# Gram stages of a two-layer bottleneck kernel: a quarter of each copy step by ScalarE, twelve transfers a step for sixteen, norms a step further ahead

## The chip, the cores and the metric

The kernel runs on one core of one Trainium2 chip. The metric is device time in microseconds (us) of one execution; the median of three runs stands for a kernel. All numbers here are from runs of this kernel on the chip and from one execution that the hardware profiler recorded.

## What is computed

Two ResNet bottleneck layers, one after the other, on x of 64 images x 1024 channels x 14 x 14 pixels (float32, 12544 pixels in all), with batch statistics taken over all images and pixels:

```python
out = relu(bn(conv(x, w1, 1x1), g1, be1))        # 1024 -> 256 channels
out = relu(bn(conv(out, w2, 3x3), g2, be2))      # 256 -> 256
out = bn(conv(out, w3, 1x1), g3, be3)            # 256 -> 1024
x = relu(x + softplus(residual_scale)[0] * out)  # then the same again with layer 1's weights
```

`bn` subtracts the mean of a channel over images and pixels, divides by sqrt(variance + 1e-5), and applies g and be.

## The kernel before, in words

The 256 channels between the convolutions live on chip in one array, `y_all`: 128 partitions, `MS` = 2 channels a partition ("slots"), 12544 pixels along the partition. The program runs in stages: the first 1x1 convolution of layer 0; for each layer the 3x3 convolution (`conv2`), then a Gram stage (`gram`, L994), then `conv3_stats` (L1099), which makes from the Gram matrix the statistics that the third normalization needs, and then the last 1x1 convolution (with layer 1's first 1x1 convolution beside it in layer 0). There are two Gram stages, one a layer.

The statistics of conv3's output, a linear map of y, follow from y's mean and its 256 x 256 Gram matrix. `gram` therefore needs y with pixels on the partitions: TensorE contracts over partitions. A `zt` tile holds 2 x 128 pixels (`CH` = 2) by 256 channels and a column of ones; six of them (`NZT`) are used in turn. Two products per 128 pixels go into the PSUM banks `cp` and `ap` (L1092, L1093), for all 49 tiles, always one tile behind the making of the tiles. A tile is made in one of two ways:

- `by_tensor` (L1035): TensorE transposes four 128 x 128 blocks into PSUM, and VectorE copies them out (L1046). The first seven tiles (`FIRST`) are made so.
- `by_vector` (L1049): VectorE transposes 32 x 32 blocks inside each group of 32 partitions (L1052). That alone would leave the pixels in groups of 32 on the wrong partitions, so the data are moved beforehand: `spread(k)` (L1024) copies a step of 1536 pixels (`STEP` = 4 runs of `RUN` = 384) from `y_all` into a buffer `home` by sixteen transfers, one for each pair (i, j): run i of the channels in partition group j goes to partition group i, column block j. Each transfer moves 32 partitions x 2 slots x 384 pixels (96 KB). Nine of the sixteen are issued by SyncE (SP), seven by GpSimd (POOL). For i = j the data keep their partitions. There are seven steps (`STEPS`), and two buffers in turn (named `ws` and `home` in layer 0, `home` twice in layer 1), so `spread(k + 2)` waits until VectorE has transposed step k. A step feeds six tiles.

Before a pixel can be used, conv2's normalization must be applied to it: `norm_to(end)` (L1012) takes the next pieces of `y_all` (`bounds`, L1006: 256, 512, 1536, 832 and then 1568 pixels) up to `end`. For each piece and slot ScalarE applies scale, shift and ReLU (`norm`, L541, its instruction is L544) and VectorE then adds a per-channel constant (`less`, L1009, L1010). Slot 1 of the first piece is done by VectorE alone (L550, L552). This is 19 ScalarE instructions in a Gram stage.

What sets the order: `pairs` (L1059) is a generator that makes tiles and calls `norm_to` and `spread` in between, at places written out by hand (`then`, L1062, during the first seven tiles; after each step's six tiles from then on). VectorE's and TensorE's instructions here keep their program order; ScalarE's norms are placed by the scheduler, which left them in program order. Each engine then runs its own queue in order: a VectorE instruction that waits for a norm holds back all VectorE work behind it, and a transfer that waits holds back those behind it on its queue. In `spread`, `norm_to(first + STEP)` comes first, so that the step's own pixels are normalized before they are moved.

The last lines that the steps of the prediction touch: L168 is the helper through which all products go; L1107 is ScalarE's first work after a Gram stage (it takes the result out of PSUM), and L331 is the helper `act`, which issues a ScalarE instruction in program order.

Of the kernel before, what the change touches and what calls it, by code (L numbers as in the profile page):

```python
# [38 lines left out]
AF = mybir.ActivationFunctionType  # L39
# [7 lines left out]
MS = M // P  # L47
# [10 lines left out]
RUN = 3 * P  # L58
STEP = 4 * RUN
# [7 lines left out]
GPX = GI * HW  # L67
# [20 lines left out]
def bottlenecks(ctx: ExitStack, tc: tile.TileContext, x, w1s, w2s, w3s, pars, out):  # L88
    nc = tc.nc
# [5 lines left out]
    y_all = keep.tile([P, MS, NPX], FP, tag="y", name="y")  # L95
# [70 lines left out]
    def matmul(*args, **kw):  # L166

        tc.keep_in_program_order(nc.tensor.matmul(*args, **kw))  # L168

    def busy(psum, tag, n, with_=None):  # L170

        v = ident if with_ is None else with_
        for i in range(n):
            matmul(psum.tile(448, tag), v, v[:, :1].to_broadcast([P, 448]), start=True, stop=True)
# [154 lines left out]
    def act(*args, **kw):  # L329

        tc.keep_in_program_order(nc.scalar.activation(*args, **kw))  # L331
# [209 lines left out]
    def norm(s, y, aff, act=nc.scalar.activation):  # L541

        scale, shift = aff
        act(y, y, AF.Relu, bias=shift[:, s : s + 1], scale=scale[:, s : s + 1])  # L544

    def norm_vector(s, y, aff, less=0.0):

        scale, shift = aff
        tc.keep_in_program_order(
            nc.vector.tensor_scalar(y, y, scale[:, s : s + 1], shift[:, s : s + 1], ALU.mult, ALU.add)  # L550
        )
        tc.keep_in_program_order(nc.vector.tensor_scalar(y, y, 0.0, less, ALU.max, ALU.add))  # L552
# [441 lines left out]
    def gram(psum, pool, homes, aff, minus_c, beside):  # L994

        g0, g1 = psum.tile(M + 1, "cp"), psum.tile(P + 1, "ap")
        zts = [pool.tile([P, CH, M + 1], FP, tag=f"zt{i}", name=f"zt{i}") for i in range(NZT)]
        for zt in zts:  # L1000
            nc.gpsimd.memset(zt[:, :, M:], 1.0)
        zts = itertools.cycle(zts)

        head = 3 * CH * P
        start = FIRST * CH * P
        bounds = [0, CH * P, head, head + STEP, *range(2 * GPX, NPX + 1, GPX)]  # L1006
        pieces = list(zip(bounds, bounds[1:]))

        def less(s, y):  # L1009
            tc.keep_in_program_order(nc.vector.tensor_scalar(y, y, minus_c[:, s : s + 1], None, ALU.add))  # L1010

        def norm_to(end):  # L1012

            while pieces and pieces[0][0] < end:
                a, e = pieces.pop(0)
                for s in reversed(range(MS)):
                    y = y_all[:, s, a:e]
                    if a == 0 and s == 1:
                        norm_vector(s, y, aff, minus_c[:, s : s + 1])
                    else:  # L1020
                        norm(s, y, aff)
                        less(s, y)

        def spread(k):  # L1024

            first = start + k * STEP if k else head
            norm_to(first + STEP)
            x = homes[k % 2][:, : MS * STEP].rearrange("p (s j f) -> p s j f", s=MS, j=4)
            for i, j in itertools.product(range(4), range(4)):
                queue = nc.gpsimd if 4 * i + j in (1, 3, 6, 8, 10, 13, 15) else nc.sync  # L1030
                a = first + i * RUN
                queue.dma_start(out=x[32 * i : 32 * i + 32, :, j], in_=y_all[32 * j : 32 * j + 32, :, a : a + RUN])
            return x.rearrange("p s j f -> p (s j) f")

        def by_tensor(a):  # L1035
            tp = psum.tile(CH * M)
            for c in range(CH):
                for s in range(MS):
                    tc.keep_in_program_order(
                        nc.tensor.transpose(  # L1040
                            tp[:, (c * MS + s) * P : (c * MS + s + 1) * P],
                            y_all[:, s, a + c * P : a + (c + 1) * P], ident,
                        )
                    )
            zt = next(zts)
            tc.keep_in_program_order(nc.vector.tensor_copy(zt[:, :, :M], tp.rearrange("p (c m) -> p c m", c=CH)))  # L1046
            return zt

        def by_vector(x, i):  # L1049
            zt = next(zts)  # L1050
            tc.keep_in_program_order(
                nc.vector.transpose(  # L1052
                    zt[:, :, :M].rearrange("p b (n c) -> p b n c", c=32),
                    x[:, :, i * CH * 32 : (i + 1) * CH * 32].rearrange("p n (b r) -> p b n r", r=32),
                )
            )
            return zt

        def pairs():  # L1059

            norm_to(head)
            then = {  # L1062
                1: lambda: ready.append(spread(0)),
                2: partial(norm_to, 2 * GPX),
                4: partial(norm_to, 3 * GPX),
                5: lambda: ready.append(spread(1)),
            }
            for i in range(FIRST):
                a = i * CH * P
                yield by_tensor(a if a < head else a + STEP)  # L1070
                if i == 0:
                    busy(psum, "ax", 1)
                if i in then:
                    then[i]()
            for k in range(STEPS):
                x = ready.pop(0)
                for i in range(RUN // (CH * 32)):
                    yield by_vector(x, i)
                if k + 2 < STEPS:
                    ready.append(spread(k + 2))  # L1080
            norm_to(NPX)
            for i in range(LAST):
                yield by_tensor(NPX - (LAST - i) * CH * P)

        ready = []
        total = NPX // (CH * P)
        before = None
        for k, zt in enumerate(itertools.chain(pairs(), (None,))):
            if before is not None:
                for c in range(CH):  # L1090
                    first, last = k == 1 and c == 0, k == total and c == CH - 1
                    matmul(g0, before[:, c, 0:P], before[:, c, :], start=first, stop=last)  # L1092
                    matmul(g1, before[:, c, P:M], before[:, c, P:], start=first, stop=last)  # L1093
            before = zt
            if k in beside:
                beside[k]()
        return g0, g1
# [133 lines left out]
    def aggregate(stats, first):  # L1231
        n = stats.shape[1]
        mv = small.tile([P, n, nc.vector.BN_AGGR_DIM], FP, tag=f"mv{n}", name="mv")
        for o in range(n):
            tc.keep_in_program_order(
                nc.vector.bn_aggr(mv[:, o, :], stats[:, o, first:, :].rearrange("p t f -> p (t f)"))
            )
        return mv
# [93 lines left out]
    with tc.tile_pool(name="first", bufs=1) as one, tc.tile_pool(  # L1332
# [5 lines left out]
        for b in range(2):  # L1338
            p = keep.tile([P, NPAR], FP, tag=f"par{b}", name=f"par{b}")
# [31 lines left out]
    for b in range(2):  # L1371
# [7 lines left out]
        with tc.tile_pool(name=f"last_{b}", bufs=1) as one, tc.tile_pool(  # L1379
# [5 lines left out]
            aff = affine(aggregate(stats2, 0), pb, G2, BE2)  # L1385
            with ExitStack() as scope:
# [4 lines left out]
                with tc.tile_pool(name=f"gram_{b}", bufs=1) as pool:  # L1391
                    def x_tile(name):
                        return xpool.tile([P, CS * PX], FP, tag="x", name=name)


                    ws = sums_tile(one, 2 - b)
                    homes = [x_tile("home") if b else ws.rearrange("p i n -> p (i n)"), x_tile("home")]

                    weights = []

                    def combined():
                        if b == 0:
                            weights.append(combine_w1(w1, ws[:, 1]))
                        weights.append(combine_w3(w3, ws[:, 0]))

                    beside = {FIRST + STEPS * RUN // (CH * 32): combined}
                    grams = gram(psum, pool, homes, aff, minus_c, beside)

                    made = [conv3(psum, 0, 0, w3, "cx" if b else "ay")]
                    mv3 = small.tile([P, CS, nc.vector.BN_AGGR_DIM], FP, tag="mv3", name="mv3")  # L1410
                    conv3_stats(psum, pool, grams, w3, mv3, ("cy", "cp", "cy", "cp" if b else "cx"), homes[1])
# [3 lines left out]
                aff = affine(mv3, pb, G3, BE3, conv_bias=B3)  # L1415
# [51 lines left out]
```

## Time and profile before

| | us |
|---|---|
| median of 3 runs | 1944.43 (1944.18 to 1944.73) |
| the profiled execution | 1944.06 |
| its span on the core | 1942.3 |
| first Gram stage, first transpose to last product | 587.8 to 659.3 |
| second Gram stage, the same | 1553.3 to 1624.3 |
| ScalarE's 19 norms in the first stage | 586.5 to 612.6 |

| 586 to 604 us | busy us of 18 | | 604 to 660 us | busy us of 56 |
|---|---|---|---|---|
| TensorE | 15.27 | | TensorE | 55.91 |
| VectorE | 15.28 | | VectorE | 38.01 |
| ScalarE | 17.51 | | ScalarE | 8.60 |
| GpSimd | 8.40 | | GpSimd | 21.75 |
| DMA engines (mean share) | 0.86 | | DMA engines (mean share) | 0.91 |

How to read the lines that follow. A line of a timeline has the start and the length in us, the engine, the line of the program, the operation, output<-input by the program's names with their shapes, and how many instructions were merged into it; what stands in brackets is how long the engine idled before it and for what. A merged line that begins with one shape may hold others. A line of a group has the count, busy us and mean ns of one, and after each bar the idle time before it. A line of waits has who waited for whom, us in total, how often, and the longest. PE is TensorE, DVE VectorE, ACT ScalarE, POOL GpSimd, SP SyncE. Sums of lengths on one engine can be over the time that they take, because neighbouring instructions overlap a little.

### The profile page before, as it was taken

Reading aid. Unit: us, or ns where it says so; the run is one execution under the profiler, and the core shown is the slowest. Engines: PE = TensorE matmul, PEld = TensorE weight load, DVE = VectorE, ACT = ScalarE, POOL = GpSimd, SP = SyncE. Lnnn points to the kernel's source line nnn. Section 1 sums busy time; section 2 is a strip of 40 time slices with the busy share of each in tenths; the row PEclk is TensorE's granted clock in tenths of the full one; section 3 lists DMA queues with packets and bytes.
Section 4 is the critical chain, followed back from the end, with each engine's and each line's share of the span. In section 5 each row is a group of like instructions: output and inputs, shape, how many; then the busy total and the mean of one; then the engine's idle time right before and its main releaser. Section 6 shows DMA issues by size and latency. Waiting matters only on the chain.

```text
span 1942.3 us, 27081 instructions
## 1 busy us (share of the span) xinstructions
PE 1918.6 (99%) x9438; PEld 1612.1 (83%) x9438; DVE 1544.3 (80%) x2473; ACT 1046.2 (54%) x2098; POOL 575.1 (30%) x674
## 2 busy tenths in 40 slices
PE   9999999999999999999999999999999999999999
PEld 5555557999997799999999999989999987555555
DVE  5778667999998667776776767689999975888886
ACT  2222214677765055555555555456777651666666
POOL 0111100212105133433333334302121051666664
PEclk9999999999999999999999999999999999999999
DMA  7777634887948634444444444258788486899998
GB/s 291 273 250 263 235 129 157 204 221 202 230 141 207 197 137 187 175 166 166 181 185 167 166 178 180 108 181 209 215 208 225 140 194 233 279 334 335 333 342 300
DMA packets 201849, 413.91 MB, mean 213 GB/s; under 512 B 37809, under 2 KB 178001, under 8 KB 185201
## 3 DMA queue, kind: packets, MB, share of 16 engines
q1 hardware_dynamic: 161728, 324.66, 49.0%
q0 software_dynamic: 34368, 36.45, 9.3%
q10 hardware_dynamic: 5616, 51.06, 6.3%
q8 instruction: 75, 1.23, 0.3%
q14 instruction: 62, 0.50, 0.1%
HBM read 263.75 MB, written 115.34 MB: 195 GB/s over the span
## 4 chain that ended last, share of the span: by engine, by line
PE 92%; DVE 5%; DMA 1%; ACT 1%; issue 1%; SPq 0%; POOL 0%; DVEq 0%; ACTq 0%
PE cy L168 17%; PE ay L168 17%; PE columns L168 13%; PE cp L168 12%; PE ap L168 10%; PE m L168 6%; PE l L168 6%; PE cx L168 5%; PE ax L168 4%; PE ps L168 1%; DMA home<-y 1%; ACT y L544 1%; DVE v L628 0%; DVE sums L622 0%; DVE steps L697 0%
## 5 line engine op out<-in xcount | busy, mean ns | idle before, releaser
L331 ACT ACTIVATE cu<-cy,scale 128x196 f32<-128x196 f32 (+1 forms) x552 | 256.7, 474 | 277.5 <-PE cy L168 271.3
L168 PE MATMUL columns<-v,ub 128*128 128x224 f32 (+1 forms) x1536 | 300.7, 337 | 0.0
L331 ACT ACTIVATE x<-x,shift 128x392 f32<-128x392 f32 x428 | 241.1, 613 | 59.5 <-POOL x L490 53.1
L168 PEld LDWEIGHTS columns<-v,ub 128*128 128x128 f32 x1536 | 269.2, 188 | 2.8
L464 DVE SCALAR_TENSOR_TENSOR x<-cp,scale,x 128x196 f32<-128x196 f32 (+1 forms) x368 | 178.2, 484 | 97.2 <-PE cp L168 96.1
L168 PE MATMUL cy<-ct,ws 128*128 128x196 f32 (+1 forms) x736 | 221.9, 383 | 1.1 <-ACT cu L331 1.1
L485 POOL TENSOR_TENSOR x<-x,cu 128x196 f32<-128x196 f32 (+1 forms) x184 | 159.3, 866 | 172.1 <-ACT cu L331 162.5
L168 PE MATMUL ay<-at,ws 128*128 128x196 f32 (+1 forms) x752 | 209.1, 381 | 0.0
L490 POOL TENSOR_TENSOR x<-x,cu 128x392 f32<-128x392 f32 x124 | 125.9, 1016 | 192.8 <-DVE x L464 188.1
L168 PEld LDWEIGHTS ay<-at,ws 128*128 128x128 f32 x752 | 136.5, 190 | 33.4
L168 PEld LDWEIGHTS cy<-ct,ws 128*128 128x128 f32 x736 | 133.3, 190 | 36.4 <-ACT cu L331 4.2
L168 PE MATMUL l<-diffs,ub 128*128 128x224 f32 (+1 forms) x768 | 149.1, 337 | 2.6 <-PE columns L168 2.6
L511 POOL TENSOR_TENSOR x<-x,cu 128x392 f32<-128x392 f32 x120 | 121.9, 1017 | 85.9 <-DVE x L464 62.4
L168 PE MATMUL m<-sums,ua 128*128 128x224 f32 (+1 forms) x752 | 145.9, 337 | 1.5 <-DVE sums L622 1.5
L168 PEld LDWEIGHTS l<-diffs,ub 128*128 128x128 f32 x768 | 134.3, 189 | 4.4 <-PE columns L168 3.9
L331 ACT ACTIVATE au<-ay 128x196 f32<-128x196 f32 (+1 forms) x141 | 53.8, 381 | 155.2 <-PE ay L168 152.4
L464 DVE SCALAR_TENSOR_TENSOR x<-cx,scale,x 128x196 f32<-128x196 f32 (+1 forms) x184 | 89.1, 484 | 57.4 <-PE cx L168 57.4
L168 PEld LDWEIGHTS m<-sums,ua 128*128 128x128 f32 x752 | 131.3, 189 | 3.3 <-DVE sums L622 2.9
L168 PE MATMUL cx<-y,w 128*128 128x196 f32 (+1 forms) x404 | 124.1, 392 | 0.4 <-DVE x L1148 0.4
L168 PE MATMUL cy<-y,w 128*128 128x196 f32 (+1 forms) x404 | 123.8, 392 | 0.0
L168 PE MATMUL cp<-zt 128*128 128x257 f32 x392 | 118.0, 382 | 1.8 <-DVE zt L1046 1.7
L168 PE MATMUL cp<-y,ws 128*128 128x196 f32 (+1 forms) x368 | 113.6, 390 | 0.9 <-DVE x L464 0.9
(216 smaller groups left out, 3924.8 us busy)
## 6 DMA issues: line engine op xcount, KB each, us to landing
x<-in_x SPq DMA_DIRECT2D x62, 1568.0 KB, 6.8
ub<-u SPq DMA_DIRECT2D x94, 768.0 KB, 5.2
x<-mid SPq DMA_DIRECT2D x32, 1568.0 KB, 8.2
mid<-x ACTq DMA_DIRECT2D x31, 1568.0 KB, 5.1
out<-x SPq DMA_DIRECT2D x123, 392.0 KB, 5.7
ua<-u SPq DMA_DIRECT2D x94, 256.0 KB, 3.0
u<-y POOLq DMA_DIRECT2D x48, 256.0 KB, 5.8
home<-y SPq DMA_DIRECT2D x90, 96.0 KB, 4.3
```

Of the source, the lines that this page charges most:

```text
L168: tc.keep_in_program_order(nc.tensor.matmul(*args, **kw))
L331: tc.keep_in_program_order(nc.scalar.activation(*args, **kw))
L464: nc.vector.scalar_tensor_tensor(v, bank, self.scale[:, o : o + 1], v, ALU.mult, ALU.add)
L485: nc.gpsimd.tensor_add(self.part(1, 1), self.part(1, 1), u3)
L490: nc.gpsimd.tensor_add(v, v, self.u12)
L511: nc.gpsimd.tensor_add(v, v, self.u12[:, i * self.n : (i + 1) * self.n])
L544: act(y, y, AF.Relu, bias=shift[:, s : s + 1], scale=scale[:, s : s + 1])
```

## The change

The transfers with i = j are no longer made. In their place a new function `stay(k)` issues four ScalarE copies, one for each group of 32 partitions (32 partitions x 2 x 384 elements each), in program order. The other twelve pairs remain transfers, seven on SyncE and five on GpSimd. ScalarE's norms go through `act` and so keep their program order too. `stay(0)` comes after the norms of the 832-pixel piece, `stay(1)` directly after `spread(1)`; for later steps the norms of one more step of pixels are put between `spread(k + 2)` and `stay(k + 2)`.

```diff
-                        norm(s, y, aff)
+                        norm(s, y, aff, act)
                         less(s, y)
 
+        def home(k):
+            return homes[k % 2][:, : MS * STEP].rearrange("p (s j f) -> p s j f", s=MS, j=4)
+
+        def first_of(k):
+            return start + k * STEP if k else head
+
+        def stay(k):
+
+            for i in range(4):
+                here, a = slice(32 * i, 32 * i + 32), first_of(k) + i * RUN
+                act(home(k)[here, :, i], y_all[here, :, a : a + RUN], AF.Copy)
+
         def spread(k):
 
-            first = start + k * STEP if k else head
+            first = first_of(k)
             norm_to(first + STEP)
-            x = homes[k % 2][:, : MS * STEP].rearrange("p (s j f) -> p s j f", s=MS, j=4)
-            for i, j in itertools.product(range(4), range(4)):
-                queue = nc.gpsimd if 4 * i + j in (1, 3, 6, 8, 10, 13, 15) else nc.sync
+            x = home(k)
+            for n, (i, j) in enumerate(itertools.permutations(range(4), 2)):
+                queue = nc.gpsimd if n in (1, 3, 6, 8, 10) else nc.sync
                 a = first + i * RUN
                 queue.dma_start(out=x[32 * i : 32 * i + 32, :, j], in_=y_all[32 * j : 32 * j + 32, :, a : a + RUN])
             return x.rearrange("p s j f -> p (s j) f")
...
                 1: lambda: ready.append(spread(0)),
-                2: partial(norm_to, 2 * GPX),
+                2: lambda: (norm_to(2 * GPX), stay(0)),
                 4: partial(norm_to, 3 * GPX),
-                5: lambda: ready.append(spread(1)),
+                5: lambda: (ready.append(spread(1)), stay(1)),
             }
...
                 if k + 2 < STEPS:
                     ready.append(spread(k + 2))
+                    norm_to(first_of(k + 2) + 2 * STEP)
+                    stay(k + 2)
```

In the built program the order on TensorE, VectorE, SyncE and GpSimd is as before, but for three things: the transfers left out, the four L1010 instead of two after the first step's six transposes, and with that none after the fourth step's (before, the last two stood there). On ScalarE, where twelve norms of 1568 pixels followed each other, there now stand: four copies, four norms, four copies, four norms, four copies, two norms, four copies, two norms, and twelve copies.

## Prediction

> **What bounds the kernel now.** I read the chain of waits first, then the two Gram stages (576 to 660 us and 1552 to 1625 us), the only ones that the edit touches. TensorE (PE) is busy 99% of the span, and the chain that ended last is 92% PE, so a Gram stage matters only where PE stands idle in it.
>
> ```profile
> PE 1918.6 (99%) x9438; PEld 1612.1 (83%) x9438; DVE 1544.3 (80%) x2473; ACT 1046.2 (54%) x2098; POOL 575.1 (30%) x674
> ...
> PE 92%; DVE 5%; DMA 1%; ACT 1%; issue 1%; SPq 0%; POOL 0%; DVEq 0%; ACTq 0%
> ```
>
> PE's waits in the first Gram stage (who, for whom, us, times, longest) are few, and none of them is for a transfer. The second stage has the same first two.
>
> ```profile
> PE cy L1040 <- DVE y L1010: 1.4, 1, 1.4
> PE cp L168 <- DVE zt L1046: 0.8, 1, 0.8
> ```
>
> The timeline of VectorE (DVE) shows why: L1010 finishes the norms that ScalarE (ACT) has begun, and the last PSUM copy (L1046, 601.88) stands behind two of them.
>
> ```profile
> 597.51 1.98 DVE L1010 TENSOR_SCALAR y<-y,minus_c 128x1568 f32<-128x1568 f32 x2
> 599.40 0.69 DVE L1046 COPY zt<-cy 128x512 f32<-128x512 f32 x1
> 600.00 1.98 DVE L1010 TENSOR_SCALAR y<-y,minus_c 128x1568 f32<-128x1568 f32 x2
> 601.88 0.69 DVE L1046 COPY zt<-ay 128x512 f32<-128x512 f32 x1
> 602.53 3.68 DVE L1052 STREAM_TRANSPOSE zt<-ws 128x512 f32<-128x512 f32 x6
> 606.13 1.94 DVE L1010 TENSOR_SCALAR y<-y,minus_c 128x1568 f32<-128x1568 f32 x2
> 611.24 3.68 DVE L1052 STREAM_TRANSPOSE zt<-home 128x512 f32<-128x512 f32 x6 [3.17 <-DMA home<-y]
> ```
>
> DVE does wait for transfers (3.17 us here). But six transposes take it 3.68 us, and PE takes six times 1.31 us (7.9 us) to use them up; that lead hides nearly all of it. PE's timeline has a product pair every 1.31 us from 602.63 on; only the starts at 612.01 and 620.25, and the ones after them, come late: 602.63 to 621.66 is 19.03 us, where 1.42 + 13 x 1.314 = 18.50 would do. So transfers cost PE 0.53 us in the first stage. In the second, all intervals after 1569.56 are 1.31 or 1.32 us: nothing.
>
> ACT's timeline, the view on which the change turns:
>
> ```profile
> 586.49 26.11 ACT L544 ACTIVATE y<-y,shift,scale 128x256 f32<-128x256 f32 x19 [1.08 <-DVE shift L1277]
> 660.02 0.28 ACT L1107 ACTIVATE g<-ap 128x129 f32<-128x129 f32 x1 [47.42 <-issue]
> ```
>
> ACT runs 19 norms without a gap up to 612.6, then idles 47 us. It is free on average, and not free in just the stretch in which PE waits for norms.
>
> [...] by the groups kept apart by shape:
>
> ```profile
> L544 ACT ACTIVATE y<-y,shift,scale 128x1568 f32<-128x1568 f32 x28 | 45.0, 1681 | 3.7 <-DVE shift L1277 3.7
> L331 ACT ACTIVATE y<-y 128x512 f32<-128x512 f32 x48 | 28.6, 625 | 57.5 <-DVE y L204 39.6 <-DVE y L201 17.6
> ```
>
> [...] Here a PE gap of 1.8 us at 1268 leaves the granted clock at 1.00; the gaps forecast below stay under 2.1 us, so I price nothing for it.
>
> **The change, part by part** (times of the first stage).
>
> *The copies.* Seven steps of four copies of 32 partitions x 2 x 384 in each stage. No row has 32 partitions. [...] so 0.84 us, and 0.745 us a copy after the overlap. Bounds: below, the 512-element copy, 0.53 us; above, the price of a norm with its two operands, 0.92 us. A gain from the copies themselves is excluded: they take ACT time where ACT has none to spare.
>
> In the built order of the changed kernel the first four stand behind the 832-pixel norms and ahead of the 1568-pixel ones. They wait for L1010 of the 1536-pixel pieces (over at 592.7) and earlier users of the buffer, so the wait costs nothing. ACT reaches them at 593.48 (586.49 + 7.64 us for seven norms - 7 x 0.093 us); they take 4 x 0.745 = 2.98 us. Behind them on ACT are the norms of pixels 3136 to 6272; for these wait L1010 on DVE, behind it the PSUM copies, behind these PE. The fourth of these norms ends at 593.48 + 2.98 + 3 x 1.588 + 1.68 = 602.90 instead of 599.92. Its L1010 starts at 602.94 instead of 600.94: about 1.0 us of the 3.0 was slack, since DVE came late to it. L1010 1.03 us, PSUM copy 0.69 us, less 0.09 us overlap: PE's last tensor-made pair starts at 604.63 instead of 602.63. **+2.0 us on the path.** In part PE waits earlier already (the transposes of 599.76 move to 600.9); that is inside the same 2.0.
>
> *Norm a step further ahead.* After the first six transposes DVE now has four L1010 (1.94 us more) instead of two, before the transposes of the second step. No DMA is in the moved step; SP and POOL aren't passed. But the four norms stand on ACT behind the second four copies: copies from 602.81 to 605.79, the last norm ends 605.79 + 3 x 1.588 + 1.68 = 612.23, its L1010 at 613.30, the first transpose (0.72 us, overlap 0.09) at 613.93, PE at 613.98. PE needs it at 604.63 + 1.42 + 6 x 1.314 = 613.93. So this second chain (eight copies deep) arrives even with the first: +0.05 us now, and beyond this point each 0.1 us more a copy costs 0.8 us a stage instead of 0.4. In later steps the copies, waiting for the transposes two steps before, have only further norms or copies behind them: the third step's norms end near 618.4, its transposes can run at 619.4, and PE needs them at about 621.1. Slack 1.7 us, growing.
>
> *Twelve transfers.* SP issues 7 instead of 9 (0.6 us each), POOL 5 instead of 7, and the DMA engines carry 1.18 MB a step instead of 1.57. For the second step they start at 600.9 (after L1010) instead of 599.5; the last run's three wait for 604.0. Before, the last issue at 604.9 landed by 611.2; now it must land by 613.2, two microseconds later and with less in flight. So nothing here is late, and the 0.53 us goes: -0.53 in the first stage, 0 in the second (bounds 0 and -0.53). If that cover failed (the third step's transfers as slow as before, 13.1 us), it would cost 0.3 us.
>
> *Sum.* First stage +2.0 + 0.05 - 0.53 = +1.5; second +2.0 + 0.05 = +2.05; total +3.6 us. Everything after a Gram stage hangs on PE's last pair (PE, then DVE's statistics, then PE again), so the shift passes to the end. The profiled execution took 1944.06 us (span 1942.3 and 1.8 around it): 1947.7. The median of the runs is 0.37 us above that execution: **1948.0 us**, +0.18%.
>
> **Rivals.** (a) *Slower clearly:* a copy costs like a norm, 0.92 us. From about 0.74 us on, the second chain decides; 8 x 0.175 = 1.4 us more a stage, 2 x 3.45 - 0.53 = +6.3: 1950.7. For it: 32-partition copies into a buffer to which DMA writes too are not in the trace. [...] (b) *No change:* DVE or the product lead has more slack than I count, or a copy takes 0.53 us; then 4 x 0.53 - 1.0 = 1.1 a stage, 2.2 - 0.53 = +1.7, or less: 1946.1 at most. For it: ACT idles 47 us. Against: it idles only after 612.6. (c) *Faster:* transfers are the true limit, as DVE's waits for home (8.5 us in the first stage, 11.1 in the second) suggest, and copies are absorbed: at most 0.53 us, 1943.9. Against: PE hardly waits for them. That the change is not as written is excluded by the built order on each engine.
>
> **Chances.** My forecast (+2.6 to +4.8, 1947.0 to 1949.2) 57%, and the line of 0.2% (3.9 us, about what a measurement of this kernel can tell from no change) runs through it: 34 below, 23 above. Rival (a) 28, slower. Rival (b) 11, same. Rival (c) 4; it gives only 0.5 us, but stands for any larger gain too. Faster 4%, same 45%, slower 51%. Range: from inside (b), 1945.8, to a little over (a), 1951.2.
>
> **What would show it.** Right: copies of about 0.84 us; the last PSUM copy near 603.9; PE's wait for it 1.8 to 1.9 us instead of 0.8; the second step's transposes near 613.2, behind L1010 and not behind DMA; no gap at 620. Wrong: copies near 1.0 us (a); PE's pair still at 602.6 to 603.7 (b); a PE wait for a transfer; a granted clock under 1.00 after the longer gap.

## The result and the profile after

The changed kernel takes **1949.03 us** (median of 10 runs, 1948.59 to 1949.68); the kernel before, beside it on the same chip, 1944.51 us (10 runs). The ratio is 1.0024, 95% interval [1.0016, 1.0033]: slower by 4.5 us. The forecast was 1948.0. The profiled execution took 1949.27 us with a span of 1947.5.

The changed kernel's page: TensorE's busy time is what it was (1919.9 against 1918.6), ScalarE has 47 us more, which is 56 copies of 0.84 us, and GpSimd 13 us less. In the chain of this page only 19% of the span is accounted for, so the chain is of no use here; the timelines have to do.

```profile
PE 1919.9 (99%) x9438; PEld 1612.5 (83%) x9438; DVE 1547.2 (79%) x2473; ACT 1093.2 (56%) x2154; POOL 561.8 (29%) x646
...
PE 18%; ACT 1%; DVE 0%; DMA 0%; SPq 0%; issue 0%
```

TensorE's waits in the first Gram stage. Before, the longest were two of 1.4 and 0.8 us; now a wait for a transpose's input has come (the second line), the wait for the last PSUM copy (L1046 before, L1058 now) is 1.5 us, and the last line is a new wait for a tile of the second step. The second stage has the same five waits, on other PSUM buffers, within 0.1 us.

```profile
PE cp L168 <- DVE zt L1058: 1.5, 1, 1.5
PE ay L1052 <- DVE y L1010: 1.5, 1, 1.5
PE cy L1052 <- DVE y L1010: 1.4, 1, 1.4
PE cy L1052 <- PE m L168: 0.5, 1, 0.5
PE cp L168 <- DVE zt L1064: 0.4, 1, 0.4
```

ScalarE's timeline, where before 19 norms stood in one line of 26.11 us:

```profile
586.86 7.08 ACT L331 ACTIVATE y<-y,shift,scale 128x256 f32<-128x256 f32 x7 [1.07 <-DVE shift L1291]
593.85 3.42 ACT L331 ACTIVATE ws<-y 32x768 f32<-32x768 f32 x4
597.28 6.46 ACT L331 ACTIVATE y<-y,shift,scale 128x1568 f32<-128x1568 f32 x4
603.64 3.42 ACT L331 ACTIVATE home<-y 32x768 f32<-32x768 f32 x4
607.09 6.45 ACT L331 ACTIVATE y<-y,shift,scale 128x1568 f32<-128x1568 f32 x4
```

Four copies take 3.42 us and the next norm starts 3.43 us after the first copy (593.85 to 597.28). One copy takes 838 ns, by the groups kept apart by shape (those into `ws`; into `home` the same):

```profile
L331 ACT ACTIVATE ws<-y 32x768 f32<-32x768 f32 x16 | 13.4, 838 | 4.6 <-DVE zt L1064 4.3
```

Four times 0.838 is 3.35: the copies don't overlap at all, there are even some 0.02 us between them. VectorE's timeline shows what follows. Before, L1010 came in pairs of 1.98 us at 597.51 and 600.00, without a wait. Now most of them wait for their norms:

```profile
599.01 1.04 DVE L1010 TENSOR_SCALAR y<-y,minus_c 128x1568 f32<-128x1568 f32 x1 [1.05 <-ACT y L331]
...
603.77 1.04 DVE L1010 TENSOR_SCALAR y<-y,minus_c 128x1568 f32<-128x1568 f32 x1 [0.53 <-ACT y L331]
604.73 0.68 DVE L1058 COPY zt<-ay 128x512 f32<-128x512 f32 x1
605.33 3.67 DVE L1064 STREAM_TRANSPOSE zt<-ws 128x512 f32<-128x512 f32 x6
608.91 1.00 DVE L1010 TENSOR_SCALAR y<-y,minus_c 128x1568 f32<-128x1568 f32 x1
...
613.57 1.04 DVE L1010 TENSOR_SCALAR y<-y,minus_c 128x1568 f32<-128x1568 f32 x1 [0.55 <-ACT y L331]
614.52 3.67 DVE L1064 STREAM_TRANSPOSE zt<-home 128x512 f32<-128x512 f32 x6
```

The last line is the second step: before, its transposes waited 3.17 us for a transfer, now the L1010 ahead of them waits for ScalarE, and the transfers are no longer waited for. In all, VectorE waited for transfers 13.5 us in the first stage before and 11.1 in the second; now 0.4 us of that is left in the first stage and none in the second. Most of its waiting is now for TensorE to give a `zt` buffer free (9.3 and 11.3 us), so VectorE is ahead there.

**Where the time went.** The measure used from here on is the start of a tile's first product on TensorE, counted from the first product of tile 0 of its stage. Tile 6 is the last that TensorE makes, tile 13 the first of the second step, tile 48 the last. Where one number stands, both stages agree within 0.02 us. The lower rows are the versions of the next section.

| kernel | tile 6 | tile 13 | tile 48, first / second stage |
|---|---|---|---|
| before | 12.90 | 22.29 / 22.20 | 68.73 / 68.18 |
| before, again | 12.91 | 22.30 / 22.54 | 68.88 / 68.63 |
| changed | 15.37 | 25.19 / 25.18 | 71.28 / 71.27 |
| changed, again | 15.39 | 25.22 / 25.21 | 71.31 / 71.30 |
| copies later | 12.90 | 25.20 | 72.66 / 72.80 |
| no norm ahead | 15.36 | 24.66 | 70.65 / 70.64 |
| both | 12.90 | 22.30 | 68.28 / 68.28 |
| copies by GpSimd | 13.57 | 22.87 | 68.86 / 68.86 |
| two copies | 13.64 | 22.94 | 68.93 / 68.94 |
| halved, reversed copies | 15.74 | 27.02 | 73.11 / 73.11 |
| one half copy a transfer | 12.90 | 24.88 | 72.60 / 72.63 |
| two half copies transfers | 12.91 | 24.56 | 70.64 / 70.65 |

The changed kernel's Gram stages are 2.55 and 3.09 us longer, 5.64 together; the medians differ by 4.5. Stage lengths are the sharper measure, and the experiments are judged by them first; the difference of about 1 us is taken up with the last pair of runs.

### The profile page after: what moved, and what is told of

It is laid out like the page before. It is cut to its first block, busy times and chain, and to the rows that moved or that the text cites. A ratio compares the mean times of both kernels' runs of the same rounds, so it can differ in the third digit from the quotient of the medians.

```text
span 1947.5 us, 27054 instructions
## 1 busy us (share of the span) xinstructions
PE 1919.9 (99%) x9438; PEld 1612.5 (83%) x9438; DVE 1547.2 (79%) x2473; ACT 1093.2 (56%) x2154; POOL 561.8 (29%) x646
## 3 DMA queue, kind: packets, MB, share of 16 engines
q8 instruction: 75, 1.23, 0.3%
```

## The experiments

**Theory.** The time is lost on two chains through ScalarE. The first has four copies in it and delays tile 6; the second has eight and delays tile 13. They are not added: the later one counts. **Rivals:** the two delays add up; or the loss is in proportion to ScalarE's work, wherever it stands; or the norms that were moved ahead are the whole loss.

*Copies later* (the first step's copies are moved behind the second step's transfers, so that the first chain is empty):

```diff
-                2: lambda: (norm_to(2 * GPX), stay(0)),
+                2: partial(norm_to, 2 * GPX),
                 4: partial(norm_to, 3 * GPX),
-                5: lambda: (ready.append(spread(1)), stay(1)),
+                5: lambda: (ready.append(spread(1)), stay(0), stay(1)),
```

> The first two steps' copies are moved behind the norms of pixels 3136 to 6272 on ScalarE; all else is as in the changed kernel. Measure: a Gram stage from its first tile's product to its last tile's, 68.7 and 68.2 us before, 71.3 and 71.3 us after. Theory (ScalarE's queue, two chains): the wait for the last PSUM copy goes back to 0.8 us and tile 6 starts 12.9 us after tile 0 instead of 15.4, but eight copies still stand ahead of the norms that were moved a step ahead, so the second step's transposes start where they did, tile 13 stays near 25.2 us, and the stages stay at 71.3 us: about +4.5 us against before, as in the changed kernel. Rival (the first four copies are the whole cost): stages of 68.2 to 69 us, within 1 us of before.

Measured: 1952.24 us (5 runs; before 1944.16), ratio 1.0039 [1.0026, 1.0051]. Tile 6 is back at 12.90, and tile 13 is at 25.20, as in the changed kernel (25.19). So emptying the first chain gives nothing at tile 13: the chains overlap, and the second alone sets the time. The rest was not expected: the stages are 1.4 to 1.5 us longer still. TensorE's single wait is now 2.74 us long, and the products after it are slow:

```profile
615.31 1.23 PE L168 MATMUL cp<-zt 128*128 128x257 f32 x2 [2.74 <-DVE zt L1064]
616.33 0.64 PE L168 MATMUL ap<-zt 128*128 128x129 f32 x2
```

A pair of cp products takes 1.23 us instead of 0.60 to 0.70. The stretches of 2 us (busy times and counts of the five engines, then the granted clock, the DMA share and GB/s) name the reason: the clock.

```profile
614.00:616.00 2.00, 0.69 (x2) 0.60 (x3) 2.00 (x4) 1.95 (x3) 0.00 (x0) 0.68 0.00 1
616.00:618.00 2.00, 2.00 (x8) 1.72 (x7) 2.00 (x4) 1.95 (x3) 0.00 (x0) 0.50 0.00 0
618.00:620.00 2.00, 2.00 (x14) 1.84 (x13) 1.26 (x2) 2.00 (x2) 1.48 (x2) 0.97 0.20 48
```

From the means 0.68 and 0.97, and 0.50 between them, the clock was at half from about 614.7 to 618.1, 3.4 us. A stage without the fall, with 1.42 us for the first tile after the wait and 1.314 for each of the others, would have its last tile at 25.20 + 1.42 + 34 x 1.314 = 71.3; it came at 72.66 and 72.80. That the number of falls differs between executions is an estimate from their means. The mean clock of the five was 0.998 in the recorded one (1952.27 us, two falls) and in that of 1952.24; it was 0.999 in those of 1950.45 and 1950.81, which are shorter by about the price of one fall, and 0.997 in that of 1953.49. Of these four there is no trace.

*No norm ahead* (the norms keep their old place, the copies stay):

```diff
                     ready.append(spread(k + 2))
-                    norm_to(first_of(k + 2) + 2 * STEP)
                     stay(k + 2)
```

> The norms are not put a step ahead; copies and transfers are as in the changed kernel. Theory: the first chain stays (tile 6 at 15.4 us after tile 0), the second step's transposes now stand behind two L1010 instead of four and start some 3 us earlier, so tile 13 comes when it is due, 24.7 us after tile 0; stages of 70.6 us, 0.6 us less each than in the changed kernel: +3.3 us against before. Rival (the norm ahead is what costs): stages of 68.2 to 68.7 us, no change against before. Rival (transfers limit the second step once the norms don't): tile 13 late and waiting for a transfer.

Measured: 1947.92 us (16 runs), ratio 1.0020 [1.0013, 1.0028]. Now the second chain is broken and the first is left alone: tile 6 at 15.36, and from there on no late start. Two waits of TensorE are those of the first chain (the rest is as before):

```profile
PE cp L168 <- DVE zt L1058: 1.5, 1, 1.5
PE ay L1052 <- DVE y L1010: 1.5, 1, 1.5
```

The first chain alone costs 15.36 - 12.90 = 2.46 us, the second alone (from the run before) 25.20 - 22.20 = 3.00; together they cost 2.98 at tile 13 (25.18 - 22.20). That is the larger of the two, not the sum. The norm ahead is not the whole loss either: without it 2.46 of 3.09 us a stage remain.

*Both edits together*, copies later and no norm ahead:

> Both edits at once: copies of the first two steps behind the norms to pixel 6272, and no norm a step ahead. Theory: both chains are gone, tile 6 at 12.9 us and tile 13 at 22.2 us after tile 0, and with twelve transfers the late starts at tiles 13 and 19 of the first stage go too: 68.2 us in both stages, 0.5 us less than before in all, 1944.0 us. Rival (something else in the copies or the twelve transfers costs, such as writes of ScalarE and of transfers to one buffer): a stage over 69 us.

Measured: 1943.08 us (13 runs; before 1944.16), ratio 0.9994 [0.9986, 1.0003]. With both chains broken only 0.10 us a stage of the loss is left, although ScalarE makes the same 56 copies. TensorE's waits are those of before:

```profile
PE cy L1052 <- DVE y L1010: 1.4, 1, 1.4
PE cp L168 <- DVE zt L1058: 0.8, 1, 0.8
```

What is left stands at tile 8, which comes 0.10 us late: the first step's transposes now wait 0.70 us for the copies themselves.

```profile
603.58 3.68 DVE L1064 STREAM_TRANSPOSE zt<-ws 128x512 f32<-128x512 f32 x6 [0.70 <-ACT ws L331]
```

This also shows what the twelve transfers gain: the first stage, 68.73 us before, is 68.28, and the late starts of tiles 19 and 20 (30.52 and 31.94 before) are gone (30.18 and 31.50); the second stage, where that execution of before has no late start, is 68.28 after 68.18. The medians say 1.1 us less than before, with an interval that holds no change. It beats the changed kernel, and isn't shown to beat the kernel before.

*Copies by GpSimd*, in the changed kernel's order:

```diff
-                act(home(k)[here, :, i], y_all[here, :, a : a + RUN], AF.Copy)
+                tc.keep_in_program_order(nc.gpsimd.tensor_copy(home(k)[here, :, i], y_all[here, :, a : a + RUN]))
```

> The same copies at the same places, but on GpSimd instead of ScalarE, whose norms then follow each other as before; the norms a step ahead stay. Theory (ScalarE's queue is what costs, not the copies, the four L1010 in a row or the twelve transfers): with GpSimd copies of some 1.3 us (an estimate from its adds, 866 ns for 196 and 1016 ns for 392 elements) the first step's are over near the time its transposes start; stages of 68.2 to 68.8 us, no change or up to 0.5 us less than before. Rival (four L1010 in a row hold VectorE too long): tile 13 late in both stages, behind L1010 that don't wait for ScalarE. A risk to both: GpSimd's copies are slower than estimated, and the transposes wait for them.

Measured: 1944.50 us (13 runs), ratio 1.0001 [0.9993, 1.0009]. ScalarE's chains are free of copies, and 4.8 of the 5.64 us go. What is late now, 0.67 us at tile 6 in both stages, is from VectorE: the pair of L1010 that runs beside GpSimd's copies takes 2.65 us, the next pair, beside none, 1.97.

```profile
597.38 2.65 DVE L1010 TENSOR_SCALAR y<-y,minus_c 128x1568 f32<-128x1568 f32 x2
...
600.55 1.97 DVE L1010 TENSOR_SCALAR y<-y,minus_c 128x1568 f32<-128x1568 f32 x2
```

GpSimd's own copies take 0.82 us by the median, not the 1.3 that was estimated (the 866 ns behind that estimate are a mean over two shapes; the adds of 196 elements alone take 780), and 1.46 us where they run beside L1010 (two of the first step's four; least, median and most in ns):

```profile
L1034 POOL COPY ws<-y x16: 814/822/1462, 596.0 to 642.7; 32x768 f32<-32x768 f32 x16
```

Side by side, the pair grew by 0.68 us and each of the two copies by 0.64; what links the two was not shown.

*Two copies* a step by ScalarE, for groups 0 and 1; the other two are transfers again (fourteen a step):

```diff
-            for i in range(4):
+            for i in range(2):
...
+            pairs = [*itertools.permutations(range(4), 2), (2, 2), (3, 3)]
-            for n, (i, j) in enumerate(itertools.permutations(range(4), 2)):
-                queue = nc.gpsimd if n in (1, 3, 6, 8, 10) else nc.sync
+            for n, (i, j) in enumerate(sorted(pairs)):
+                queue = nc.gpsimd if n in (1, 3, 6, 8, 10, 12) else nc.sync
```

> Only the two groups i = 0, 1 are copied by ScalarE; (2, 2) and (3, 3) are transfers again, fourteen a step. My theory: two chains lead through ScalarE; the first has four copies in it and 1.0 us of slack, the second has eight and decides in the changed kernel. With half the copies (two take about 1.71 us) the first makes tile 6 late by 1.71 - 0.97 = 0.74 us: first product of tile 6 at 13.64 us from the stage's first product (before 12.90, changed kernel 15.37); the second chain has 3.4 us less in it and isn't felt: tile 13 at 13.64 + 9.25 = 22.9 (changed kernel 25.19); last tile at 68.9 in both stages (up to 69.4 in the first if fourteen transfers still come late). Sum +0.9 us, about 1945.4 to 1945.8, within 0.1% of before. Rival: the loss is ScalarE's time, in proportion: half the copies cost half of the 5.6 us, last tile at 69.8 in both stages, 1947.3.

Measured: 1944.85 us (13 runs; before 1944.16), ratio 1.0004 [0.9996, 1.0012]. Tile 6 is at 13.64 and the last tile at 68.93 and 68.94, as the theory had them; the median is below the 1945.4 to 1945.8 that was expected. With half of ScalarE's copies the two stages are 0.96 us longer than before, not half of 5.64: the loss is a chain beyond its slack, not a share of work. And fourteen transfers are as good as twelve: no late start at tile 19.

*Halved and reversed copies.* Why do the copies not overlap? Here they stand in the order of groups 3, 2, 1, 0, each as two copies of one slot:

```diff
-            for i in range(4):
+            for i in reversed(range(4)):
...
-                act(home(k)[here, :, i], y_all[here, :, a : a + RUN], AF.Copy)
+                for s in range(MS):
+                    act(home(k)[here, s, i], y_all[here, s, a : a + RUN], AF.Copy)
```

> The four copies of a step stand in the order of groups 3, 2, 1, 0, and each is two copies, one a slot (32 partitions x 384): eight copies of about 0.51 us. The question is why copies of the changed kernel follow each other at 0.865 us although each takes 0.838, while the norm ahead of them overlaps its first copy by 0.10. Theory: an instruction overlaps with the next only if both begin at the same partition (norms begin at partition 0, as does the first copy). Then the two copies of a group follow at about 0.51 - 0.09 = 0.42 us, a copy of the next group at about 0.53; the norm ahead doesn't overlap its first copy (group 3), and the last copy (group 0) overlaps with the norm behind. Rival: an instruction of 32 partitions never overlaps with its successor: all follow at about 0.53 us, the norm ahead overlaps its first copy, the norm behind doesn't overlap. Eight copies take about 3.8 us (theory) or 4.2 us (rival), so the stages are longer than in the changed kernel by about 0.8 to 1.6 us each, if the second chain decides.

The starts of ScalarE's instructions in the first step's copies, from the trace. Beside them the changed kernel's; "overlap" is the end of one minus the start of the next:

| changed: pair of neighbours | overlap, us | halved, reversed: pair | overlap, us |
|---|---|---|---|
| norm, group 0 | 0.09 | norm, group 3 | -0.02 |
| groups 0, 1 | -0.02 | group 3, 3 | 0.09 |
| groups 1, 2 | -0.03 | groups 3, 2 | -0.02 |
| groups 2, 3 | -0.02 | group 2, 2 | 0.09 |
| group 3, norm | -0.01 | groups 2, 1 and 1, 0 | -0.02 |
| norm, norm | 0.09 | group 0, norm | 0.09 |

The theory holds at each pair: an instruction overlapped with the next by 0.09 us where both begin at the same partition (a norm of all 128 partitions begins where group 0 does), and where they don't the next began 0.01 to 0.03 us after the end. Whether there are 32 or 128 partitions played no part: the overlap is 0.09 us in pairs of either kind. As a kernel this order is worse (1953.51 us, one run; the stages 1.8 us longer than in the changed kernel, where 0.8 to 1.6 were expected): the eight copies take 3.80 us, and group 3, now first, waits for the step's last pixels (1.10 us on ScalarE at 605.5).

```profile
594.25 3.81 ACT L331 ACTIVATE ws<-y 32x384 f32<-32x384 f32 x8
597.96 6.44 ACT L331 ACTIVATE y<-y,shift,scale 128x1568 f32<-128x1568 f32 x4
605.51 3.80 ACT L331 ACTIVATE home<-y 32x384 f32<-32x384 f32 x8 [1.10 <-DVE y L1010]
```

*Which gap lowers the clock?* Two versions have a gap between the one after which the clock stayed (1.8 and 1.9 us, halved and reversed copies) and the one after which it fell (2.74). Both are "copies later" with half of a copy made a transfer again, in the second step only (`(1,)`) or in the first two (`(0, 1)`):

```diff
-                act(home(k)[here, :, i], y_all[here, :, a : a + RUN], AF.Copy)
+                s = slice(0, 1 if i == 3 and k in (1,) else MS)
+                act(home(k)[here, s, i], y_all[here, s, a : a + RUN], AF.Copy)
...
+            if k in (1,):
+                a = first + 3 * RUN
+                nc.sync.dma_start(out=x[96:128, 1, 3], in_=y_all[96:128, 1, a : a + RUN])
```

> As with both steps' copies behind the second step's transfers (there TensorE stood idle for 2.73 us, twice, and both times the granted clock fell to half for some 3.4 us afterwards, which made the stage about 1.36 to 1.5 us longer), but half of one copy of the second step (group 3, slot 1) is a transfer again. That copy falls from 0.84 to 0.51 us, so TensorE's gap before tile 13 should be 2.73 - 0.33 = 2.40 us. If the length of the gap decides and the limit lies below 2.4 us, the clock falls again and the stage is 72.3 us long; if it lies above, the clock stays at 1.00 and the stage is 68.28 + 2.40 + 0.10 + 0.1 = 70.9 us.

> The same, with that half copy a transfer in the first step too: gap 2.73 - 0.66 = 2.07 us. If the limit lies between 1.81 us (a gap after which the clock was seen to stay) and 2.07, the clock falls and the stage is about 72.0 us; otherwise it stays and the stage is about 70.55 us.

Measured: the first has gaps of 2.41 and 2.42 us, and the clock fell in both stages (72.60 and 72.63; 1952.7 us, one run). The second has gaps of 2.19 and 2.20 us, 0.12 longer than worked out, and the clock stayed (70.64 and 70.65; 1948.39 us, one run). Two kernels that differ by half a copy in the first step are thus 4 us apart, in one execution each. The stretches of the first, then of the second:

```profile
614.00:616.00 2.00, 0.69 (x2) 0.60 (x3) 2.00 (x4) 1.95 (x3) 0.00 (x0) 0.82 0.01 3
616.00:618.00 2.00, 2.00 (x8) 1.72 (x7) 2.00 (x4) 1.95 (x3) 0.00 (x0) 0.50 0.00 0
```

```profile
614.00:616.00 2.00, 1.26 (x7) 1.15 (x8) 2.00 (x5) 1.95 (x3) 0.00 (x0) 1.00 0.00 0
616.00:618.00 2.00, 2.00 (x14) 1.84 (x13) 1.65 (x3) 1.97 (x3) 0.06 (x1) 1.00 0.00 0
```

In the recordings of "copies later" and of these two, 4 of 4 gaps of 2.41 us or more lowered the clock, and 2 of 2 of about 2.2 did not. That doesn't yet make the length of the gap the cause, because the falls keep a beat of their own. These are the times at which they begin, in us, found with narrow stretches; the third is behind the last product:

| version | first | second | third | distances |
|---|---|---|---|---|
| copies later | 614.73 | 1584.11 | 1949.34 | 969.38, 365.23 |
| one half copy a transfer | 615.27 | 1584.65 | 1949.88 | 969.38, 365.23 |

The distances are 284 and 107 times 3.4133 us (969.38 / 284 and 365.23 / 107), and 3.41 us is the length of one fall. So in these two executions the falls begin at the marks of one period, and not at a fixed time after a gap begins: in the first stage 2.16 us after it in the one, 2.38 in the other. In the period ahead of each fall in a stage TensorE had been idle for 2.16 and 2.45 us (copies later), 2.38 and 2.41 us (one half copy). With two half copies the marks, counted back from the fall at the end of the program (1945.46 us), cut both gaps of 2.2 us: no period holds more than 1.7 us of them. Behind the last product both kernels show the same. Before, TensorE ends at 1937.69 us and the clock falls at 1942.95, 5.26 us later; changed, at 1943.26 and 1947.81, 4.55 later. One period ahead of these falls lie marks that come 1.85 and 1.14 us after the last product, and there the clock stayed at 1.00.

Idle time within a period thus sorts these gaps as well as the length of a gap does: up to 1.85 us without a fall, 2.16 us or more with one. It would also let a gap of 2.74 us pass without a fall where a mark cuts it, and that fits the shorter executions of "copies later" (1950.45 and 1950.81 us). No run here puts one and the same gap at another place in the period, so which of the two decides is open, and that a gap of 2.2 us never lowers the clock is not shown.

*Both kernels again.* Outside of the Gram stages one step sets the execution of before apart from all others: at 1344 us, in layer 1's 3x3 convolution, TensorE waits 0.57 us for VectorE (L622), 0.21 in the others. Both kernels were recorded a second time, unchanged.

> The kernel before, recorded a second time. Outside of the Gram stages one step of 0.35 us separates the recorded execution of before from those of six other versions: TensorE waits 0.57 us at 1344 us for VectorE's sums (L622), against 0.21 in the others. If this belongs to an execution and not to the kernel, the second recording may show 0.21 us there, and 896.4 us instead of 896.8 from the last tile of the first Gram stage to the first of the second; if it belongs to the kernel before (its order or its places in memory), it shows 0.57 again and 896.8. The tiles within the Gram stages should be as before: 12.90 for tile 6, 68.7 and 68.2 us for tile 48.

> The changed kernel, recorded a second time, for the same question: 0.21 us and 896.4 us again if it belongs to the kernel, either value if it belongs to the execution. Within the Gram stages 15.37 us for tile 6, 25.19 for tile 13 and 71.28 us for tile 48, since these follow from chains within the stage.

Measured: 1945.06 and 1949.03 us (one run each). The step belongs to the kernel: 0.6 us again for before, 0.2 again for the changed one. In the window from 1341 to 1351 us, before again:

```profile
PE m L168 <- DVE sums L622: 0.6, 1, 0.6
```

and the changed kernel again:

```profile
PE m L168 <- DVE sums L622: 0.2, 1, 0.2
```

So 0.36 us is given back there, by every version that holds part of the edit (0.21 or 0.22 us in all ten traces); why VectorE's sums come earlier, far from any edited line, I haven't found. The stages of the changed kernel repeat to 0.03 us, as chains of fixed lengths should. Those of before do not: tile 19 is late again (0.15 us more), and in the second stage tile 13 now comes late (an interval of 1.65 us instead of 1.32, and 1.42 for the next). What transfers cost before thus varies with the execution: 0.5 us in the one, 0.7 and 0.45 (68.88 - 68.18 and 68.63 - 68.18) in the other. Against this second recording the changed kernel's stages are 5.1 us longer. A second piece is given back behind TensorE's last product: from there to the end of the span it is 4.59 and 4.60 us in the two recordings of before, 4.23 in both of the changed kernel. What makes it I haven't found; among the other versions it is 4.22 to 4.60. So 5.1 to 5.6, less 0.36 and 0.37, leaves 4.4 to 4.9, beside 4.5 in the medians. On top of that, single executions differ ahead of the first Gram stage, where the first products wait for their first transfers: its first tile starts at 589.60 us in the earliest recording and at 590.43 in the latest.

## Why the prediction was right, and which term was off

The direction, the mechanism and both chains were as predicted; the size was about 1 us short in the median and 1.5 to 2.1 us short in the stages (5.1 to 5.64 against 3.55). The stages alone lie outside the forecast of +2.6 to +4.8; that the median lies inside it is luck, as the sum below shows.

- **"No row has 32 partitions ... so 0.84 us"**: right, 838 ns. The 0.84 was my estimate; rows of the trace of before give it too, 625 ns for a copy of 512 and, by the norms of 832 (1066 ns, the line below) and of 1568 (1681), (1681 - 1066) / 736 = 0.836 ns an element: 625 + 256 x 0.836 = 839.

```profile
L544 ACT ACTIVATE y<-y,shift,scale 128x832 f32<-128x832 f32 x4 | 4.1, 1066 | 0.0
```

- **"and 0.745 us a copy after the overlap"**: this is the term that failed. Neighbouring norms overlap by 0.09 us (measured), and I took that for the copies too. But the copies change their partitions each time, and none of them overlaps: 3.43 us for four instead of 2.98, 0.86 us a copy as the path feels it. Every number that follows from the copies is short for this one reason.
- **"+2.0 us on the path"** (first chain): 2.46 measured, alone and in the changed kernel. 2.0 + 0.45 = 2.45. The slack of 1.0 us was right (3.43 - 2.46 = 0.97). The last PSUM copy came at 604.73, predicted near 603.9: 0.45 of the difference is the copies, 0.38 the later start of this execution's stage.
- **"+0.05 us, and beyond this point each 0.1 us more a copy costs 0.8 us a stage"** (second chain): the place and the slope were right, the point was passed: the second step's transposes started at 614.52, predicted near 613.2, behind L1010 as forecast. At 0.86 us a copy, eight copies are 8 x 0.115 = 0.92 us later than priced: 2.05 + 0.92 = 2.97 at tile 13, measured 2.98. The chain that I called even with the first is the one that decides; the run with the first chain emptied shows it. A further 0.10 us a stage was missing: after a wait the next tile takes 1.42 us instead of 1.31 (tile 14), which makes 3.09.
- **"-0.53 in the first stage, 0 in the second"** (twelve transfers): right for the execution that I read, and somewhat small as a price of the kernel: in the other recording it is 0.7 and 0.45. With both chains broken the late starts are gone in both stages.
- **PE's wait for the last PSUM copy, "1.8 to 1.9 us"**: 1.5. Most of the delay came ahead of it, with a wait of 1.5 us for a transpose's input, which I had put at 1.1 us of delay (599.76 to 600.9): tile 5 starts at 12.28 instead of 10.51, 1.77 late, and the last copy adds only 0.69, which makes the 2.46.
- **"I price nothing for it"** (the clock): right here, since the longest gap in a Gram stage is 1.5 us. The reason given was too generous: the trace of before showed the clock at 1.00 after a gap of 1.8 us, and that it would stay so up to 2.1 us was my estimate; in "one half copy a transfer" it fell after gaps of 2.41 us. Had both chains' delay fallen into one gap, as in "copies later", the change would have cost up to the 8 us measured there.
- **Sum**: +1.5 and +2.05 were forecast, 2.55 and 3.09 measured. With 0.86 us for 0.745 the prediction's own working gives 2.97 - 0.53 = 2.4 and 3.0. That the median is nevertheless only 1.0 us over the forecast is luck: it is owed to things that the forecast did not hold, 0.36 us given back in the 3x3 convolution, some 0.37 behind the last product, and the transfers' higher price in another execution of before.
- **Rivals**: (a) was named as "a copy costs like a norm, 0.92 us". It does not, but its consequence, the second chain deciding, came true with the overlap as the cause. (b), more slack than counted, and (c), transfers as the limit, are refuted: the first by the slack of 0.97 us, the second by VectorE's transfer waits, which went from 24.6 us in the two stages to 0.4 while the stages grew by 5.1 us or more. What these waits had cost TensorE before is at most 1.15 us (0.7 + 0.45).

## What to carry to other kernels

An engine's mean load says nothing on whether it can take more: ScalarE at 54% was full for just the 26 us in which others waited for it, and the same copies cost 2.5 to 3 us a stage in that stretch and 0.1 us behind it, when the norms too kept their place. Count how many of the new instructions stand ahead of each thing that is waited for, against the slack of that chain; of several chains that end at the same engine the later one counts, not their sum (here 2.46 and 3.00 us alone, 2.98 together). An overlap between neighbours that a trace shows for one kind of instruction need not hold for another on the same engine (0.09 us between the norms, none between the copies): look at what changes from one instruction to the next before it is taken over.

## What the runs showed of the hardware that was not expected

- In the changed kernel and with halved, reversed copies, ScalarE's neighbouring instructions overlapped by 0.09 us where they begin at the same partition, and only there. Copies on partitions 0, 32, 64 and 96 in turn followed each other 0.02 us after the end (pitch 0.865 us at 0.838 us of length).
- TensorE's granted clock fell to 0.50 for 3.41 us after idle gaps of 2.41 to 2.74 us, in both stages of two recorded executions; after gaps of 2.2 us and less it stayed at 1.00. The falls of these two executions begin at the marks of a period of 3.413 us (distances of 284 and 107 periods), those in a stage after a period with 2.16 to 2.45 us of idling; after 1.85 us behind the last product (before) none began. Whether the gap's length or the idling within a period decides is open. A fall cost an estimated 1.4 to 1.7 us (stages of 72.66 and 72.80 against 71.3; of 72.60 and 72.63 against 24.88 + 1.42 + 34 x 1.314 = 71.0).
- VectorE's tensor-scalar instructions of 128 x 1568 and GpSimd's copies of 32 x 768 took longer side by side (copies by GpSimd): 2.65 us instead of 1.97 for two of the first, 1.46 instead of 0.82 for one of the second. Six of VectorE's transposes, with GpSimd's copies beside them from 604.26 us on, took 3.66 us (from 603.04), against 3.68 before.
